# Graph attention, layer 0: 16 of 22 chunks of weights turned in blocks by VectorE, adjacency masks on ScalarE, ragged chunks of both heads turned together

## The chip, the cores and the metric

One core of one Trainium2 chip. The metric is the device time of one execution in microseconds, from runs of the whole program; the kernel before has a median of 2697.96 us over 3 runs (2696.49 to 2704.17).

## The reference, cut to what matters

Four graph layers over x (2708 x 512, float32) and an adjacency matrix (2708 x 2708, ones and zeros with ones on the diagonal). The change touches layer 0 alone, attention with 8 heads of 64:

```python
adj = jnp.maximum(adjacency_matrix, jnp.eye(n))
keys    = jnp.einsum('nj,hjk->hnk', node_matrix, Wks)      # queries, values alike
atts = jnp.einsum('hqk,hmk->hqm', queries, keys) / key_dim ** 0.5
atts = atts - 1e+16 * (1.0 - adj)[None, :, :]
atts = jax.nn.softmax(atts, axis=-1)
return jnp.einsum('hqm,hmk,hko->qo', atts, values, Wo)
```

Then `x = layernorm(x + layer(x, adj))`, and likewise for layers 1 to 3 (a normalised product with the adjacency, an additive attention, and a second normalised product). Layer 1 and layer 3 need the row sums of the adjacency, which layer 0 gathers on its way.

## The kernel before, in words

The 2708 rows are cut into 22 chunks of 128, the last with 20 rows. Keys (`KT`), values (`V`) and queries are computed first; the queries go to DRAM (`qtd`). Then one loop runs over 88 items: 22 chunks of query rows times 4 pairs of heads. `Pair` (L266) holds one item's state.

The keys of one item are taken in three batches, `ends = [0, 7, 14, 22]` in chunks, so 896, 896 and 916 columns. The steps of an item are:

- `scores(k, part)` (L283): half a batch; two TensorE products (one for each head) into PSUM `pss`, and for each head one VectorE pass (L306) that adds the mask from the adjacency tile, writes the scores to `s` and keeps the row maximum in `mx`. There are two `pss` banks for each head.
- `maxima` (L317): the negative row maximum `nm`, VectorE.
- `weights(k)` (L323): the exponential in place in `s` with its row sum, ScalarE, one instruction for each head (L328).
- The weights must then be turned, so that keys lie on partitions. For the first 14 chunks (`ND`) VectorE turns 32 x 32 blocks from `s` to `d` (`blocks`, L336) and `deal` (L348) moves the blocks to their partitions with four DMAs from `d` to `e` on SyncE's queue. To fit the order of keys that this gives, the rows of `V` of these chunks are permuted when they are projected (`xp`, GpSimd).
- `turn` (L359) does the last 8 chunks on TensorE: a transpose of each chunk of each head into PSUM `pst`, and copies to `pt` on ScalarE. The last, ragged chunk goes to `lastT`, which has zeros below its 20 rows.
- `values(m0, m1)` (L383): the products of the weights with `V` into PSUM `av`; after the 22nd chunk a copy to `ot` on ScalarE, and a store by GpSimd.

The adjacency of the next chunk of rows is loaded (`load_chunk`), summed by ScalarE (`row_sums`), and made into the mask (`mask`): VectorE puts ones on the diagonal where the batch holds it and turns 1 and 0 into 0 and -1e16. This is done in three of the four items of each chunk (`prep`).

The order of TensorE, VectorE and ScalarE inside the loop is the order in which the program writes it (`tc.manual_schedule`); SyncE's queue of DMAs is ordered by the framework. In one turn of the loop four items are in work: `new` gets scores, `cur` gets weights and is turned, `late` gets the products of the last batch and of the first, and `old` those of the second batch. `heads_sums` and `heads_rows` collect the reciprocals of the softmax sums twice in the whole loop.

The tiles `d` and `e` come from one pool `dep` with 3 buffers each; `s` has 5 buffers, `pt` 2, `pst` 3.

Of the kernel before, what the change touches and what calls it, by code (L numbers as in the profile page):

```python
# [15 lines left out]
P = 128  # L16
# [6 lines left out]
def kernel(  # L23
# [90 lines left out]


    NW = 3
    ends = [0, 7, 14, NC]
    ND = 14
    KD4 = P // 32
    SW = max(min(b * P, N) - a * P for a, b in zip(ends, ends[1:]))  # L120
    dgp = const.tile([P, NC, NW], F32, tag="dgp", name="dgp")
    nc.vector.memset(dgp, 0.0)
    HALF0 = NC // 2
# [7 lines left out]
    with ExitStack() as l0:  # L131
# [39 lines left out]
                a[:q, n0 : n0 + w], a[:q, n0 : n0 + w], AF.Copy, accum_out=dgp[:q, c, k : k + 1]  # L171
            )

        def mask(c, k):

            r0, q = rows(c)
            a = loaded[c][0]
            n0, w = batch(k)
            if n0 <= r0 < n0 + w:
                nc.vector.tensor_tensor(a[:q, r0 : r0 + q], a[:q, r0 : r0 + q], ident[:q, :q], ALU.max)  # L180
            nc.vector.tensor_scalar(a[:q, n0 : n0 + w], a[:q, n0 : n0 + w], 1.0, 1e16, ALU.subtract, ALU.mult)

        with tc.tile_pool(name="kvw", bufs=1) as kvw, tc.tile_pool(name="xTb", bufs=2) as xtp, tc.tile_pool(
            name="ps_0", bufs=4, space=PSUM
# [5 lines left out]
            for b in range(NB):  # L190
                n0, w = cols(b)
                xb = xtp.tile([P, KC, BLK], F32, tag="xb", name=f"xb{b}")
                load_rows(xb[:, :, :w], xT[:, n0 : n0 + w])
                if b == 0:
                    load_rows(wv_sb, wv)
                    load_rows(wq_sb, wq)

                def project_in(w_sb, p, name):
                    ps = ps_0.tile([P, BLK], F32, tag="t", name=name)
                    for k in range(KC):  # L200
                        nc.tensor.matmul(  # L201
                            ps[:, :w],
                            w_sb[:, k, p * P : (p + 1) * P],
                            xb[:, k, :w],
                            start=(k == 0),
                            stop=(k == KC - 1),
                        )
                    return ps

                for p in range(NP):  # L210
                    ps = project_in(wk_sb, p, f"psk{b}_{p}")
                    evac(KT[:, p, n0 : n0 + w], ps[:, :w])


                xp = xtp.tile([P, KC, BLK], F32, tag="xp", name=f"xp{b}", bufs=1)
                for c in chunks_of(b):
                    o, q = rows(c)[0] - n0, rows(c)[1]
                    src = xb[:, :, o : o + q]
                    dst = xp[:, :, o : o + q]
                    if c < ND:  # L220
                        src = src.rearrange("p k (i x) -> p k x i", i=KD4)
                        dst = dst.rearrange("p k (x i) -> p k x i", i=KD4)
                    nc.gpsimd.tensor_copy(dst, src)
                for c in chunks_of(b):
                    r0, q = rows(c)
                    ps = ps_0.tile([P, BLK], F32, tag="t", name=f"psv{c}")
                    for k in range(KC):
                        nc.tensor.matmul(  # L228
                            ps[:q, :],
                            xp[:, k, r0 - n0 : r0 - n0 + q],  # L230
                            wv_sb[:, k, :],
                            start=(k == 0),
                            stop=(k == KC - 1),
                        )
                    evac(V[:q, c, :], ps[:q, :])
                qb = xtp.tile([P, NP, BLK], F32, tag="qb", name=f"qb{b}")
                for p in range(NP):
                    ps = project_in(wq_sb, p, f"psq{b}_{p}")
                    nc.scalar.mul(qb[:, p, :w], ps[:, :w], QSCALE)
                for c in chunks_of(b):  # L240
                    r0, q = rows(c)
                    nc.gpsimd.dma_start(qtd[c], qb[:, :, r0 - n0 : r0 - n0 + q])
                if b == NB - 3:
                    for k in range(NW + 1):
                        load_chunk(0, k)
                    for k in range(NW):
                        row_sums(0, k)
                        mask(0, k)

            ga_sb = kvw.tile([P, D], F32, tag="ga", name="ga_sb")  # L250
# [9 lines left out]
        ps_a = l0.enter_context(tc.tile_pool(name="ps_a", bufs=1, space=PSUM, reuse_waits="tile"))  # L260
        ps_s = l0.enter_context(tc.tile_pool(name="ps_s", bufs=2, space=PSUM, reuse_waits="tile"))
        sp = l0.enter_context(tc.tile_pool(name="sp", bufs=5, reuse_waits="tile"))
        dep = l0.enter_context(tc.tile_pool(name="dep", bufs=3, reuse_waits="tile"))
        ptp = l0.enter_context(tc.tile_pool(name="ptp", bufs=2, reuse_waits="tile"))

        class Pair:  # L266

# [65 lines left out]
                        accum_out=smt[c // HALF0][:q, c % HALF0, 2 * p + j, k : k + 1],  # L333
                    )

            def blocks(self, k, j, m0, m1):  # L336

                if k not in self.D:
                    n = ends[k + 1] - ends[k]
                    self.D[k] = dep.tile([P, KD4, 2, n, 32], F32, tag="d", name=f"d{self.c}_{self.p}_{k}")  # L340
                b = 32 * self.groups
                m0, m1 = m0 - ends[k], m1 - ends[k]
                nc.vector.transpose(  # L343
                    self.D[k][:b, :, j, m0:m1].rearrange("p i m x -> p m i x"),
                    self.s[k][:b, j, m0 * P : m1 * P].rearrange("p (m i x) -> p m i x", i=KD4, x=32),
                )

            def deal(self, k):  # L348

                n = ends[k + 1] - ends[k]  # L350
                e = dep.tile([P, KD4, 2, n, 32], F32, tag="e", name=f"e{self.c}_{self.p}_{k}")
                for g in range(self.groups):
                    nc.sync.dma_start(
                        e[:, g].rearrange("p j m x -> p (j m x)"),
                        self.D[k][32 * g : 32 * g + 32].rearrange("p i j m x -> p i (j m x)"),
                    )
                self.E[ends[k]] = e

            def turn(self, m0, m1):  # L359

                c, p, q = self.c, self.p, self.q
                k = max(k for k in range(NW) if ends[k] <= m0)
                tiles = []
                for j in range(2):
                    pt = ps_t.tile([P, 4, P], F32, tag="t", name=f"pst{c}_{p}_{m0}_{j}")
                    n = sum(rows(m)[1] == P for m in range(m0, m1))
                    sb = ptp.tile([P, n, P], F32, tag=f"pt{n}", name=f"pt{c}_{p}_{m0}_{j}")
                    full = 0
                    for i, m in enumerate(range(m0, m1)):
                        mr = rows(m)[1]  # L370
                        o = (m - ends[k]) * P
                        nc.tensor.transpose(pt[:mr, i, :q], self.s[k][:q, j, o : o + mr], ident[:q, :q])  # L372
                        full += mr == P
                    if full:
                        nc.scalar.copy(sb[:, :full, :q], pt[:, :full, :q])  # L375
                    if full < m1 - m0:
                        mr = rows(m1 - 1)[1]
                        nc.scalar.copy(lastT[:mr, j, :q], pt[:mr, full, :q])
                    tiles.append(sb)
                for i, m in enumerate(range(m0, m1)):  # L380
                    self.pts[m] = (tiles, i)

            def values(self, m0, m1):  # L383
                c, p, q = self.c, self.p, self.q
# [2 lines left out]
                for m in range(m0, m1):  # L387
                    for j in range(2):
                        h = 2 * p + j
                        if m < ND:  # L390
                            f = max(f for f in self.E if f <= m)
                            x = self.E[f][:, :, j, m - f, :] if q == P else self.E[f][:, 0, j, m - f, :q]
                        else:
                            tiles, i = self.pts[m]
                            x = tiles[j][:, i, :q] if rows(m)[1] == P else lastT[:, j, :q]
                        nc.tensor.matmul(  # L396
                            self.av[j * KD : (j + 1) * KD, :q],
                            V[:, m, h * KD : (h + 1) * KD],
# [36 lines left out]
        with tc.manual_schedule(  # L435
            engines={mybir.EngineType.PE, mybir.EngineType.DVE, mybir.EngineType.Activation}
        ):
            for i in range(len(items) + 3):
# [9 lines left out]
                    new.scores(0, 0)  # L448
                    new.scores(0, 1)
                if old is not None:  # L450
                    old.values(7, ND)
                if cur is not None:
                    cur.weights(1)
                    cur.blocks(0, 0, 0, 7)
                    cur.blocks(0, 1, 0, 7)
                    cur.deal(0)
                if new is not None:
                    new.scores(1, 0)
                    new.scores(1, 1)
                if cur is not None:  # L460
                    cur.weights(2)
                if late is not None:
                    late.values(14, NC)
                    late.values(0, 7)
                if prep:
                    row_sums(c + 1, p - 1)
                if cur is not None:
                    cur.blocks(1, 0, 7, ND)
                    cur.blocks(1, 1, 7, ND)
                    cur.deal(1)  # L470
                if prep:
                    mask(c + 1, p - 1)
# [4 lines left out]
                if i in (HALF0 * NP + 2, len(items) + 1):  # L477
                    sums = heads_sums(i > HALF0 * NP + 2)
                if cur is not None:
                    cur.turn(14, 18)  # L480
                    cur.turn(18, NC)
                if i in (HALF0 * NP + 2, len(items) + 1):
                    heads_rows(*sums)
                old, late, cur = late, cur, new

# [598 lines left out]
```

## Time and profile before

| | |
|---|---|
| median of 3 runs | 2697.96 us |
| profiled execution, its own time | 2692.39 us |
| its span, first to last instruction | 2690.6 us |
| granted TensorE clock, mean | 0.992 |
| TensorE busy | 2630.5 us, 98% |
| VectorE busy | 1768.0 us, 66% |
| ScalarE busy | 1212.0 us, 45% |
| GpSimd busy | 330.5 us, 12% |
| 400 to 600 us: TensorE, VectorE, ScalarE busy | 200.0, 185.7, 152.3 us |
| 400 to 600 us: DMA share, GB/s | 0.72, 188 |

The page of a profile gives busy times of the engines, then the span in 40 slices with the busy share of each in tenths. Groups are listed by source line, engine and operation, with count, busy time, mean duration of one, and the idle time just before them with what ended it. The chain of waits follows the work that ended last back from the end, piece by piece: start, duration, engine, tile, line and number of instructions. A float32 product appears as two records, a transpose as one. PE is TensorE, PEld its loading of weights, DVE is VectorE, ACT ScalarE, POOL GpSimd, SP SyncE. The attention loop of layer 0 runs from about 233 to 1309 us of the span.

### The profile page before, as it was taken

To read this page: it belongs to the slowest core of one execution; us is meant where nothing else is said; L and a number is where in the kernel's file an instruction comes from. 1 tells how busy PE (TensorE), PEld (TensorE's weight loads), DVE (VectorE), ACT (ScalarE), POOL (GpSimd) and SP (SyncE) were. 2 spreads that over 40 slices of the span, in tenths; PEclk is the share of its full clock that TensorE was granted. 3 is DMA by queue.
4 is the path that set the end of the run, shared out by engine and by line. 5 is a ranking of instruction groups with operands and counts; after the bars stand their busy time and mean duration, and the time that the engine had idled before them with its cause. 6 is when DMAs were issued, how large, how long until landed. Compare 5 with 4: busy or idle time off the path is not lost.

```text
span 2690.6 us, 42656 instructions
## 1 busy us (share of the span) xinstructions
PE 2630.5 (98%) x15594; PEld 1484.2 (55%) x15594; DVE 1768.0 (66%) x4438; ACT 1212.0 (45%) x2570; POOL 330.5 (12%) x336
## 2 busy tenths in 40 slices
PE   8999999999999999999899999899999999999998
PEld 3445666666666666666547444444444464444445
DVE  2005999999999999999684677987776851111112
ACT  1114777777777777777311001565665530000001
POOL 1110000000000000001320000243333420000000
PEclk9999999999999999999899999999999999999999
DMA  5013777777767777776572444454433122222221
GB/s 193 32 52 76 206 182 186 202 186 190 198 177 204 184 181 207 181 186 148 151 234 66 131 123 140 126 165 127 138 114 100 49 59 69 77 78 77 78 67 41
DMA packets 199617, 361.98 MB, mean 135 GB/s; under 512 B 25160, under 2 KB 121752, under 8 KB 199408
## 3 DMA queue, kind: packets, MB, share of 16 engines
q1 hardware_dynamic: 193104, 342.52, 47.4%
q0 software_dynamic: 6304, 16.74, 1.8%
q8 instruction: 123, 2.02, 0.3%
q14 instruction: 86, 0.70, 0.1%
HBM read 186.36 MB, written 16.73 MB: 75 GB/s over the span
## 4 chain that ended last, share of the span: by engine, by line
PE 82%; issue 10%; DVE 4%; DMA 2%; ACT 1%; POOL 1%; SPq 1%; POOLq 0%; ACTq 0%; DVEq 0%
PE acc L641 19%; PE pss L298 16%; PE av L396 16%; PE acc L747 7%; PE pst L372 6%; PE pf L653 3%; PE psv L228 3%; PE psk L201 3%; PE psq L201 3%; PE po L587 2%; PE ph L733 2%; PE p L778 1%; PE pz L653 1%; DVE s L306 1%; DVE d L343 1%
## 5 line engine op out<-in xcount | busy, mean ns | idle before, releaser
L306 DVE CUSTOM_DVE_ANT_0 s<-pss,adj 128x448 f32<-128x448 f32 (+3 forms) x1056 | 596.3, 620 | 77.1 <-PE pss L298 75.4
L328 ACT ACTIVATE s<-s,nm 128x896 f32<-128x896 f32 (+1 forms) x528 | 546.9, 1038 | 12.6 <-DVE nm L321 12.4
L298 PE MATMUL pss<-KT,qt 64*128 64x448 f32 (+3 forms) x2112 | 478.0, 566 | 2.0 <-DVE mx L306 2.0
L641 PE MATMUL acc<-at,x 128*128 128x512 f32 (+1 forms) x1008 | 387.2, 542 | 0.0
L343 DVE STREAM_TRANSPOSE d<-s 128x896 f32<-128x896 f32 (+1 forms) x352 | 369.6, 1088 | 1.1 <-ACT s L328 1.1
L641 PE MATMUL acc<-pt,x 128*128 128x512 f32 (+1 forms) x880 | 336.6, 542 | 13.2 <-ACT pt L694 9.7
L396 PE MATMUL av<-e,V 128*64 128x128 f32 (+1 forms) x4928 | 300.3, 273 | 0.0
L396 PEld LDWEIGHTS av<-e,V 128*64 128x64 f32 x4928 | 267.9, 139 | 56.0 <-issue 45.5
L641 PEld LDWEIGHTS acc<-at,x 128*128 128x128 f32 x1008 | 180.8, 190 | 204.9 <-issue 202.6
L298 PEld LDWEIGHTS pss<-KT,qt 64*128 64x128 f32 (+1 forms) x2112 | 182.0, 182 | 156.0 <-issue 100.3
L641 PEld LDWEIGHTS acc<-pt,x 128*128 128x128 f32 x880 | 159.5, 194 | 189.9 <-issue 163.5
L375 ACT COPY pt<-pst 128x512 f32<-128x512 f32 (+3 forms) x352 | 165.4, 522 | 204.6 <-PE pst L372 204.2
L747 PE MATMUL acc<-at,h 128*128 128x512 f32 (+1 forms) x504 | 196.8, 543 | 0.0
L705 POOL TENSOR_TENSOR cs<-cs,pt 128x512 f32<-128x512 f32 (+2 forms) x110 | 156.6, 1423 | 202.5 <-ACT pt L694 195.9
L372 PEld LDWEIGHTS pst<-ident,s 128*128 128x128 f32 (+3 forms) x1408 | 140.4, 135 | 73.1 <-issue 58.3
L372 PE MATMUL pst<-ident,s 128*128 128x128 f32 (+3 forms) x1408 | 177.2, 277 | 1.7 <-ACT pt L375 1.4
L407 POOL DMA_DIRECT2D otd<-ot x88 | 47.4, 538 | 982.5 <-ACT ot L406 969.5
L396 PEld LDWEIGHTS av<-pt,V 128*64 128x64 f32 x2464 | 131.6, 139 | 60.5 <-ACT s L328 55.7
L692 DVE TENSOR_TENSOR pt<-pt,at 128x512 f32<-128x512 f32 (+2 forms) x132 | 107.0, 818 | 76.8 <-ACT pt L691 76.7
L93 ACT ACTIVATE ln_t<-lnve 128x1 f32<-128x1 f32 x88 | 17.7, 201 | 310.1 <-DVE lnve L107 309.9
L396 PE MATMUL av<-pt,V 128*64 128x128 f32 (+1 forms) x2464 | 152.3, 275 | 3.9 <-ACT ot L406 3.9
L1014 DVE TENSOR_TENSOR y<-z,x 128x512 f32<-128x512 f32 (+1 forms) x22 | 15.2, 692 | 211.0 <-ACT z L1012 210.9
(164 smaller groups left out, 2774.0 us busy)
## 6 DMA issues: line engine op xcount, KB each, us to landing
e<-d SPq DMA_DIRECT2D x680, 224.0 KB
at<-in_adjT_dram SPq DMA_DIRECT2D x315, 256.0 KB
a<-in_adj_dram SPq DMA_DIRECT2D x38, 677.0 KB
adj<-in_adj_dram SPq DMA_DIRECT2D x42, 448.0 KB
adj<-in_adj_dram SPq DMA_DIRECT2D x21, 458.0 KB
rb<-rs_d SPq DMA_DIRECT2D x44, 128.0 KB
qtd<-qb POOLq DMA_DIRECT2D x21, 256.0 KB, 5.2
qt<-qtd SPq DMA_DIRECT2D x21, 256.0 KB
```

The lines of the kernel that those rows point to most:

```text
L201: nc.tensor.matmul(ps[:, :w], w_sb[:, k, p * P : (p + 1) * P], xb[:, k, :w], start=(k == 0), stop=(k == KC - 1),)
L298: nc.tensor.matmul(pss[j][:q, :hw], qt[j * KD : (j + 1) * KD, p, :q], KT[j * KD : (j + 1) * KD, p, n0 + h0 : n0 + h0 + hw], start=True, st ...
L306: nc.vector.tensor_tensor_reduce(out=s[:q, j, h0 : h0 + hw], in0=pss[j][:q, :hw], in1=a[:q, n0 + h0 : n0 + h0 + hw], scale=1.0, scalar=LOW ...
L328: nc.scalar.activation(self.s[k][:q, j, :w], self.s[k][:q, j, :w], AF.Exp, bias=nm[j][:q], accum_out=smt[c // HALF0][:q, c % HALF0, 2 * p ...
L343: nc.vector.transpose(self.D[k][:b, :, j, m0:m1].rearrange("p i m x -> p m i x"), self.s[k][:b, j, m0 * P : m1 * P].rearrange("p (m i x) - ...
L372: nc.tensor.transpose(pt[:mr, i, :q], self.s[k][:q, j, o : o + mr], ident[:q, :q])
L375: nc.scalar.copy(sb[:, :full, :q], pt[:, :full, :q])
L396: nc.tensor.matmul(self.av[j * KD : (j + 1) * KD, :q], V[:, m, h * KD : (h + 1) * KD], x, start=(self.done == 0), stop=(self.done == NC - 1),)
L641: nc.tensor.matmul(acc[k][:, :w], last[0][g : g + mr, :] if m == NC - 1 else values[:mr, k * P : (k + 1) * P], moving[g : g + mr, :w], sta ...
L653: nc.tensor.matmul(pz[:q, :], yt[:, k, i * P : i * P + q], w_sb[:, k, :], start=(k == 0), stop=(k == KC - 1))
L705: nc.gpsimd.tensor_tensor(sums[:mr, :w], sums[:mr, :w], pt[:mr, :w], ALU.add)
L747: nc.tensor.matmul(acc[hc][:, :w], lastH[g : g + mr, :] if m == NC - 1 else H[m][:mr, hc * P : (hc + 1) * P], at[g : g + mr, :w], start=(m ...
```

## The change

- The batches become 8, 8 and 6 chunks (`ends = [0, 8, 16, NC]`): 1024, 1024 and 660 columns. `blocks` and `deal` now do 16 chunks, 8 to a batch; `turn` does the last 6.
- `turn` makes three PSUM tiles in place of four: four full chunks for each head, then one tile with the fifth full chunk of both heads and the ragged chunk of both heads. ScalarE copies it with one copy for the full chunks and one for `lastT`, where each head had its own.
- `mask` is an activation on ScalarE (Identity, scale 1e16, bias the tile `far` of -1e16). The ones on the diagonal stay on VectorE in a step of their own, `loops`.
- In the loop, `row_sums` moves ahead of `weights(1)`, `loops` comes after the first `blocks`, and `mask` stays after the second. `heads_rows` of the first half comes one turn later.
- `d` and `e` get pools of their own: `d` with 2 buffers where it had 3, `e` with 3 as before.

```diff
-    ends = [0, 7, 14, NC]
-    ND = 14
+    ends = [0, 8, 16, NC]
+    ND = ends[2]
...
+    far = const.tile([P, 1], F32, tag="far", name="far")
+    nc.vector.memset(far, -1e16)
...
-        def mask(c, k):
+        def loops(c, k):
...
             if n0 <= r0 < n0 + w:
                 nc.vector.tensor_tensor(a[:q, r0 : r0 + q], a[:q, r0 : r0 + q], ident[:q, :q], ALU.max)
-            nc.vector.tensor_scalar(a[:q, n0 : n0 + w], a[:q, n0 : n0 + w], 1.0, 1e16, ALU.subtract, ALU.mult)
+
+        def mask(c, k):
+
+            q = rows(c)[1]
+            n0, w = batch(k)
+            a = loaded[c][0][:q, n0 : n0 + w]
+            nc.scalar.activation(a, a, AF.Identity, scale=1e16, bias=far[:q])
...
-        dep = l0.enter_context(tc.tile_pool(name="dep", bufs=3, reuse_waits="tile"))
-        ptp = l0.enter_context(tc.tile_pool(name="ptp", bufs=2, reuse_waits="tile"))
+        dp = l0.enter_context(tc.tile_pool(name="dp", bufs=2, reuse_waits="tile"))
+        ep = l0.enter_context(tc.tile_pool(name="ep", bufs=3, reuse_waits="tile"))
+        ptp = l0.enter_context(tc.tile_pool(name="ptp", bufs=1, reuse_waits="tile"))
...
+            def turn(self):
 
                 c, p, q = self.c, self.p, self.q
...
+                last = NC - 2
+                o, mr = (NC - 1 - ND) * P, rows(NC - 1)[1]
+
+                def part(j, m):
+                    return self.s[2][:q, j, (m - ND) * P : (m - ND) * P + P]
+
                 for j in range(2):
...
+                    pt = ps_t.tile([P, last - ND, P], F32, tag="t", name=f"pst{c}_{p}_{j}")
+                    sb = ptp.tile([P, last - ND, P], F32, tag="pt", name=f"pt{c}_{p}_{j}", bufs=2)
+                    for m in range(ND, last):
+                        nc.tensor.transpose(pt[:, m - ND, :q], part(j, m), ident[:q, :q])
+                    nc.scalar.copy(sb[:, :, :q], pt[:, :, :q])
...
+                pt = ps_t.tile([P, 4, P], F32, tag="t", name=f"pst{c}_{p}_2")
+                sb = ptp.tile([P, 2, P], F32, tag="pt2", name=f"pt{c}_{p}_2")
+                for j in range(2):
+                    nc.tensor.transpose(pt[:, j, :q], part(j, last), ident[:q, :q])
+                for j in range(2):
+                    nc.tensor.transpose(pt[:mr, 2 + j, :q], self.s[2][:q, j, o : o + mr], ident[:q, :q])
+                nc.scalar.copy(sb[:, :, :q], pt[:, :2, :q])
+                nc.scalar.copy(lastT[:mr, :, :q], pt[:mr, 2:, :q])
...
                 if old is not None:
-                    old.values(7, ND)
+                    old.values(ends[1], ND)
+                if prep:
+                    row_sums(c + 1, p - 1)
                 if cur is not None:
                     cur.weights(1)
-                    cur.blocks(0, 0, 0, 7)
-                    cur.blocks(0, 1, 0, 7)
+                    cur.blocks(0, 0)
+                    cur.blocks(0, 1)
                     cur.deal(0)
+                if prep:
+                    loops(c + 1, p - 1)
...
                 if late is not None:
-                    late.values(14, NC)
-                    late.values(0, 7)
-                if prep:
-                    row_sums(c + 1, p - 1)
+                    late.values(ND, NC)
+                    late.values(0, ends[1])
                 if cur is not None:
-                    cur.blocks(1, 0, 7, ND)
-                    cur.blocks(1, 1, 7, ND)
+                    cur.blocks(1, 0)
+                    cur.blocks(1, 1)
                     cur.deal(1)
                 if prep:
                     mask(c + 1, p - 1)
...
                 if cur is not None:
-                    cur.turn(14, 18)
-                    cur.turn(18, NC)
-                if i in (HALF0 * NP + 2, len(items) + 1):
+                    cur.turn()
+                if i in (HALF0 * NP + 3, len(items) + 1):
                     heads_rows(*sums)
```

More of the change, by code (lines that the diff above doesn't have):

```diff
@@ L247 @@
                         row_sums(0, k)
+                        loops(0, k)
                         mask(0, k)
@@ L334, in weights, with blocks @@
                     )
-            def blocks(self, k, j, m0, m1):
+            def blocks(self, k, j):
                 if k not in self.D:
                     n = ends[k + 1] - ends[k]
-                    self.D[k] = dep.tile([P, KD4, 2, n, 32], F32, tag="d", name=f"d{self.c}_{self.p}_{k}")
+                    self.D[k] = dp.tile([P, KD4, 2, n, 32], F32, tag="d", name=f"d{self.c}_{self.p}_{k}")
                 b = 32 * self.groups
-                m0, m1 = m0 - ends[k], m1 - ends[k]
+                n = ends[k + 1] - ends[k]
                 nc.vector.transpose(
-                    self.D[k][:b, :, j, m0:m1].rearrange("p i m x -> p m i x"),
-                    self.s[k][:b, j, m0 * P : m1 * P].rearrange("p (m i x) -> p m i x", i=KD4, x=32),
+                    self.D[k][:b, :, j].rearrange("p i m x -> p m i x"),
+                    self.s[k][:b, j, : n * P].rearrange("p (m i x) -> p m i x", i=KD4, x=32),
                 )
@@ L350, in deal @@
                 n = ends[k + 1] - ends[k]
-                e = dep.tile([P, KD4, 2, n, 32], F32, tag="e", name=f"e{self.c}_{self.p}_{k}")
+                e = ep.tile([P, KD4, 2, n, 32], F32, tag="e", name=f"e{self.c}_{self.p}_{k}")
                 for g in range(self.groups):
@@ L357, in deal @@
                 self.E[ends[k]] = e
-            def turn(self, m0, m1):
+            def turn(self):
                 c, p, q = self.c, self.p, self.q
-                k = max(k for k in range(NW) if ends[k] <= m0)
-                tiles = []
+                last = NC - 2
+                o, mr = (NC - 1 - ND) * P, rows(NC - 1)[1]
+                def part(j, m):
+                    return self.s[2][:q, j, (m - ND) * P : (m - ND) * P + P]
                 for j in range(2):
[L365 to L381, printed above, removed]
@@ new lines, in turn @@
+                    pt = ps_t.tile([P, last - ND, P], F32, tag="t", name=f"pst{c}_{p}_{j}")
[3 more added lines that the diff above has]
+                    nc.scalar.copy(sb[:, :, :q], pt[:, :, :q])
+                    for m in range(ND, last):
+                        self.pts[m, j] = sb[:, m - ND, :q]
@@ L383, in values @@
+                for j in range(2):
+                    self.pts[last, j] = sb[:, j, :q]
+                    self.pts[NC - 1, j] = lastT[:, j, :q]
             def values(self, m0, m1):
@@ L393, in values @@
                         else:
-                            tiles, i = self.pts[m]
-                            x = tiles[j][:, i, :q] if rows(m)[1] == P else lastT[:, j, :q]
+                            x = self.pts[m, j]
                         nc.tensor.matmul(
```

## The prediction

> **What bounds the kernel now.** The page's first two parts place the stage: layer 0 fills roughly slices 4 to 19 of 40, and there TensorE and VectorE both show 9s. A 98% busy TensorE need not be the bound, so I read next the chain of waits in the middle of the stage; one period of it (one pair of heads of one row chunk):
>
> ```profile
> 505.26 1.98 PE pst L372 x16
> 507.23 1.71 PE pss L298 x8
> 508.94 1.68 PE av L396 x28
> 510.62 1.71 PE pss L298 x8
> 512.32 3.42 PE av L396 x60
> 515.75 1.74 PE pss L298 x8
> 517.49 1.98 PE pst L372 x16
> ```
>
> Every piece is TensorE and each begins where the last ended: 12.23 us, with no other engine and no wait in it. By kind: scores 5.16, values 5.10, transposes 1.98. Then the groups of the stretch 300 to 1100 us, split by shape (65.4 periods), and its waits:
>
> ```profile
> L343 DVE STREAM_TRANSPOSE d<-s 128x896 f32<-128x896 f32 x261 | 274.2, 1089 | 0.0
> L328 ACT ACTIVATE s<-s,nm 128x896 f32<-128x896 f32 x263 | 271.6, 1035 | 0.0
> L372 PE MATMUL pst<-ident,s 128*128 128x128 f32 x910 | 125.7, 281 | 0.0
> L375 ACT COPY pt<-pst 128x512 f32<-128x512 f32 x130 | 69.8, 589 | 155.2 <-PE pst L372 155.2
> L181 DVE TENSOR_SCALAR adj<-adj 128x896 f32<-128x896 f32 x33 | 19.8, 599 | 0.4
> ...
> DVE s L306 <- PE pss L298: 57.2, 66, 1.4
> ```
>
> VectorE is the near second: its only real idle time is 57.2 us, 0.87 us a pair, always at the first scores of a pair. ScalarE is busy about 9.3 us of 12.2 (the windows: 152.3 of 200) and waits for the transposes of TensorE. The timeline shows how the two leaders meet:
>
> ```profile
> 602.47 0.63 DVE L181 TENSOR_SCALAR adj<-adj 128x896 f32<-128x896 f32 x1
> 603.01 2.04 PE L372 MATMUL pst<-ident,s 128*128 128x128 f32 x16
> 604.98 1.77 PE L298 MATMUL pss<-KT,qt 64*128 64x448 f32 x8
> 605.23 0.28 DVE L321 TENSOR_REDUCE nm<-mx 128x1 f32<-128x6 f32 x2
> 606.03 0.62 DVE L306 CUSTOM_DVE_ANT_0 s<-pss,adj 128x448 f32<-128x448 f32 x1 [0.53 <-PE pss L298]
> 608.22 2.10 DVE L343 STREAM_TRANSPOSE d<-s 128x896 f32<-128x896 f32 x2
> ```
>
> VectorE has ended its maxima at 605.51 and idles to 606.03, because TensorE spent 603.01 to 604.98 on `turn`'s 16 transposes and only then began the scores. The first two periods of the stage, before TensorE has values to multiply, last 11.65 and 11.46 us (starts of the block transposes): what VectorE alone would set.
>
> **What the skill says.** VectorE: DVE Perf Modes, section on the TRN2 errata, gives fp32 two-tensor work as (N+151)/0.96 ns. 896 columns make 1091; the trace has 1089 for the block transpose, so I use that slope (1.04 ns a column). ScalarE: Activation LUTs, "What ACT_TABLE_LOAD costs", gives 280 ns + 0.833 ns a column with a bias operand, 93 ns of it overlapped back to back: 1026 for 896 against 1035 here. Its "Table sets" says that identity and copy are filler in every set, so the mask should bring no table load; before runs no Identity, so no line shows it. TensorE: Matmul & The Clock Gate, "PE-mode transpose", has about 275 ns for one transpose in a kernel; here 281 each, but 16 of them overlap into 1.98 us, so the price I use is 0.124 us.
>
> **The change, part by part**, for one pair.
> TensorE. `turn` covers 6 chunks for 2 heads, 12 transposes for 16: 4 x 0.124 = 0.495 us less, on the path. Scores keep 12 multiplications and 2 x 2708 columns; bursts of 448 and 458 columns (1.71, 1.74) give 0.87 ns a column and head pair, so 512 makes 1.93 a burst and 330 makes 1.29: 5.15 for 5.16. Values keep 88 records (32 + 56 for 28 + 60). Period 11.75.
> VectorE. 12 score passes: the spacing at 448 is 0.545 us, so 0.612 at 512 and 0.422 at 330: 6.58 before and after. Four block transposes go from 1.05 (2.10 for two) to 1.183: +0.53. This width isn't in the trace; bounds are 1.05 (no growth) and 1.25 (a fifth more), I take the slope. The mask, 0.53 in three pairs of four, goes; `loops` keeps 0.28 in one of four. Sum 6.58 + 4.73 + 0.28 = 11.59, or 11.87 with `loops`; it was 11.06, and 11.6 to 11.9 with the mask.
> ScalarE. Six exponentials keep their columns. Copies: from 2 of 512 columns, 2 of 384, 2 of 20 partitions to 2 of 512, one of 256, one of 20 partitions: about -0.7. Mask: an activation without accumulator, 1.04 (1024) or 0.74 (660) by the skill's price, bounds 0.6 (VectorE's) and 1.15; +0.7 on average. Near zero in sum, under slack of some 3 us. What matters is order: `row_sums`, 1.13 us, now precedes `weights(1)`.
>
> Stepping one pair from TensorE's start at 604.98: scores to 606.91, values to 608.77, scores to 610.70, values to 613.95, scores to 615.24, transposes to 616.73. VectorE: first pass 606.12, scores to 608.57, blocks to 610.94, scores to 613.39, blocks to 615.76, scores and maxima to 617.73; the next scores reach it at 617.87. It idles 0.14. The next score bank is free at 616.60, 0.13 before TensorE wants it. ScalarE: `weights(0)` ends about 608.05 (wanted 608.57), copy of `ot` 609.16, `row_sums` 610.29, `weights(1)` 612.57 (wanted 613.39), `weights(2)` 614.25 (wanted by the transposes 615.24), mask 615.3, copies from 615.97. Behind the moved `row_sums` stand both later exponentials and so the second block transpose, with 0.8 us to spare; its adjacency piece lands a whole pair earlier (624.9 to 627.8, wanted about 633). So TensorE stays ahead, but by a hair: the pair with `loops` is 0.14 over and hand-offs cost 0.1 to 0.2 each. I put 0 to 0.11 us a pair for that, 0.06 taken.
> SyncE and DMA. Still 8 deals a pair and the same loads; each deal grows from 224 to 256 KB. The DMA share of 0.74 becomes about 0.85 (deals are 79% of the bytes, the period 4% shorter). `d` has two buffers for three: `blocks(0)` now waits for the deal of one pair earlier. Matching landing records to issues, a batch of four deals has landed 6.9 us (median) after its block transpose, 8.05 at the 95th percentile. Scaled by bytes that is 7.9 and 9.2; the room is 11.8 - 2.4 = 9.4. So a few waits under 1 us, about +2 us in all (0 to 10).
> Nothing for: the projections' extra permuted chunks on GpSimd (TensorE's unbroken 13.7 us bursts there hide it), chunk 0's mask on ScalarE (14% busy there), the `far` memset. `heads_rows` moved a pair later removes one 1.7 us wait for `ri`, and its store on GpSimd's queue is wanted only after the stage; the end's first weight load gets a wait for ScalarE: -1 and +1.
>
> Sum: 86 pairs (the first two are VectorE's) x -0.495 = -42.6; +5 lag; +2 deals; 0 at the ends: -35.6. Against the profiled execution's own 2692.4 us (span 2690.6) this is 2656.8; the median shown is 5.6 above it, so 2662.4, said as **2662**. Its own range is 2652 (all 43 us and the small wait) to 2675.
>
> **The rivals.**
> VectorE becomes the bound. For it: only 0.14 us of slack. At 1.25 us a transpose it needs 11.93 with `loops` spread, period near 12.0: 86 x 0.22 = 19 us, 2679. At 1.33 it eats all: 2698. Against: the slope fits 448 and 896 columns within 1%. Chance 0.18, a third of it within 0.3%.
> The third `d` buffer was needed: slower. If a batch lands L after its transpose, VectorE can't start the next sooner, so the period is at least L + 2.4 + 0.1. It decides from L = 9.7; at 10.3 the period is 12.8 and 86 x 0.57 gives +49, 2747. For it: the DMA queues show 9s for most of a period, chunk loads (1.6 MB) push in front, bursts at 9.5 occur. Against: L must grow by 40% where bytes grow by 14%. Chance 0.08.
> ScalarE's order bites (`weights(0)` ending 0.2 us before VectorE wants it, `row_sums` late): 0.1 to 0.3 us a pair back, 2670 to 2688. Chance 0.10, mostly still faster.
> That the change isn't what it says is excluded by the instruction order: 12 transposes a pair, masks on ScalarE.
>
> **How the numbers follow.** The forecast has 0.64. A change under 0.3% (8 us) is about what this measurement can't tell from none. Faster: 0.64 + 0.12 + 0.08 = 0.84; same: 0.06 + 0.02 = 0.08; slower: 0.08. The range takes in the forecast's and most of the VectorE and ScalarE cases: 2649 to 2690.
>
> **What would show it.** Right: in the chain of waits `pst` x12 at 1.49 us, `pss` of 1.93, 1.93 and 1.29, period 11.75 to 11.85, still all TensorE; VectorE's wait for `pss` down from 0.87 us to 0.1 to 0.3 a pair; transposes at 1.22 us; no new wait of `d` for a DMA. Wrong: VectorE pieces in the chain, TensorE waiting for `mx` or `d`, block transposes waiting for `e`'s DMA or for exponentials, or a changed length outside layer 0.

## The result, and the profile after

| | before | after |
|---|---|---|
| median, measured side by side | 2697.22 us (4 runs) | 2662.1 us (4 runs, 2657.45 to 2663.44) |
| ratio, 95% interval | | 0.9867 [0.9838, 0.9895] |
| profiled execution, its span | 2692.39, 2690.6 us | 2662.35, 2660.6 us |
| transposes, scores, values of a pair | 1.98, 5.16, 5.10 us | 1.46, 5.15, 5.11 us |
| period, median | 12.23 us | 11.72 us |
| mean of 80 periods in the steady loop | 12.280 us | 11.855 us |
| last product of the attention ends | 1318.2 us | 1287.7 us |

The kernel is 35.1 us faster by the medians and 30.0 us by the two profiled executions. On another chip (e10 below) the ratio was 0.9891 [0.9869, 0.9913], 31 us. The period here and below is the distance between the starts of a pair's first block transposes; the first three and the last pairs are left out of the mean. Two profiles of the changed kernel, this one and e10's, differ by 0.033 us in the mean, 2.6 us over 80 pairs: differences between profiles that are smaller than this say nothing.

The chain of waits in the middle of layer 0, one period of the kernel after (start, duration, engine, tile, line, number):

```profile
510.91 1.02 PE pst L382 x8
511.94 0.22 PE pst L389 x2
512.16 0.22 PE pst L391 x2
512.38 1.92 PE pss L308 x8
514.29 1.90 PE av L410 x32
516.19 1.92 PE pss L308 x8
518.11 3.21 PE av L410 x56
521.32 1.31 PE pss L308 x8
522.63 1.02 PE pst L382 x8
```

It still holds nothing but TensorE, and each piece begins where the last ended: 522.63 - 510.91 = 11.72 us. Transposes are 1.46 us where they were 1.98; scores and values are what they were. The groups of the stretch 300 to 1060 us, by shape (count | busy us, mean ns | idle before):

```profile
L353 DVE STREAM_TRANSPOSE d<-s 128x1024 f32<-128x1024 f32 x256 | 302.9, 1222 | 8.5 <-DMA e<-d 4.4 <-ACT ot L420 2.7 <-issue 1.3
...
L383 ACT COPY pt<-pst 128x512 f32<-128x512 f32 x129 | 69.4, 589 | 92.1 <-PE pst L382 91.9
...
L189 ACT ACTIVATE adj<-adj,far 128x1024 f32<-128x1024 f32 x32 | 36.3, 1135 | 0.0
```

The block transpose takes 1222 ns, as the slope foretold, and it has idle time before it, which it didn't have before (0.0). The masks are on ScalarE at 1135 ns, and ScalarE still idles before its first copy: 92.1 us, 1.4 us a pair. The waits of VectorE (us in all, times, longest), over the attention loop:

```profile
DVE s L316 <- PE pss L308: 28.6, 60, 4.7
DVE d L353 <- DMA e<-d: 4.7, 6, 1.3
DVE d L353 <- ACT ot L420: 2.7, 4, 0.9
```

and the first of these lines before:

```profile
DVE s L306 <- PE pss L298: 75.4, 83, 4.5
```

New is that the block transposes wait: for the deals to be done with `d`. Two more lines put 2.1 us of such waits down to exponentials and 1.3 us to issue. What they really wait for comes out when the landing records of the deals are matched to their issues: from 280 to 1200 us, 14 block transposes idle for more than 0.1 us, and each of the 14 starts 0.12 to 0.18 us after the deals of one pair earlier have landed, whichever engine the list blames. Each comes 12 to 18 us after the loads of the next adjacency and queries were issued in one burst. One of these waits lies on the chain that ended last, at 713 us:

```profile
713.33 0.23 PE pst L391 x2
...
716.72 4.01 DMA e<-d
...
723.15 2.28 DVE d L353 x2
...
725.89 2.40 PE pss L308 x8
```

The chain leaves TensorE, goes through a deal on the DMA queue, and comes back by VectorE's scores and block transposes to TensorE, whose next scores take 2.40 us where they take 1.92 otherwise. The timeline of VectorE names the moment:

```profile
718.36 2.37 DVE L353 STREAM_TRANSPOSE d<-s 128x1024 f32<-128x1024 f32 x2 [1.19 <-DMA e<-d]
```

### The profile page after: what moved, and what is told of

Its sections match the earlier page's. It is cut to its first block, busy times and chain, and to the rows that moved or that the text cites. A ratio compares the mean times of both kernels' runs of the same rounds, so it can differ in the third digit from the quotient of the medians.

```text
span 2660.6 us, 41510 instructions
## 1 busy us (share of the span) xinstructions
PE 2599.1 (98%) x15242; PEld 1469.1 (55%) x15242; DVE 1772.1 (67%) x4373; ACT 1231.4 (46%) x2460; POOL 331.8 (12%) x336
## 3 DMA queue, kind: packets, MB, share of 16 engines
q8 instruction: 121, 1.98, 0.3%
## 4 chain that ended last, share of the span: by engine, by line
PE 76%; issue 10%; DVE 6%; DMA 3%; SPq 2%; ACT 2%; POOL 1%; POOLq 0%; DVEq 0%; ACTq 0%
PE acc L656 20%; PE pss L308 15%; PE av L410 14%; PE acc L762 7%; PE pf L668 3%; PE psv L236 3%; PE psk L209 3%; PE pst L382 3%; PE psq L209 3%; DVE s L316 2%; DVE d L353 1%; PE ph L748 1%; DMA e<-d 1%; PE p L793 1%; PE pz L668 1%
## 5 line engine op out<-in xcount | busy, mean ns | idle before, releaser
L316 DVE CUSTOM_DVE_ANT_0 s<-pss,adj 128x512 f32<-128x512 f32 (+3 forms) x1056 | 594.5, 618 | 29.9 <-PE pss L308 28.6
L338 ACT ACTIVATE s<-s,nm 128x1024 f32<-128x1024 f32 (+1 forms) x528 | 546.3, 1037 | 25.5 <-DVE nm L331 24.5
L308 PE MATMUL pss<-KT,qt 64*128 64x512 f32 (+3 forms) x2112 | 487.2, 568 | 7.3 <-DVE mx L316 7.0
L353 DVE STREAM_TRANSPOSE d<-s 128x1024 f32<-128x1024 f32 (+1 forms) x352 | 416.4, 1221 | 11.0 <-DMA e<-d 4.7
L410 PEld LDWEIGHTS av<-e,V 128*64 128x64 f32 x5632 | 306.7, 139 | 66.0 <-issue 35.5
L410 PE MATMUL av<-e,V 128*64 128x128 f32 (+1 forms) x5632 | 339.0, 273 | 0.0
L707 DVE TENSOR_TENSOR pt<-pt,at 128x512 f32<-128x512 f32 (+2 forms) x132 | 107.2, 819 | 75.4 <-ACT pt L706 75.4
L383 ACT COPY pt<-pst 128x512 f32<-128x512 f32 (+1 forms) x176 | 92.1, 572 | 128.2 <-PE pst L382 128.1
L762 PEld LDWEIGHTS acc<-at,h 128*128 128x128 f32 x504 | 90.2, 190 | 101.4 <-issue 99.2
L410 PEld LDWEIGHTS av<-pt,V 128*64 128x64 f32 x1760 | 93.6, 138 | 69.7 <-ACT adj L172 46.2
L709 ACT ACTIVATE pt<-pt 128x512 f32<-128x512 f32 (+2 forms) x132 | 76.2, 579 | 109.2 <-DVE pt L708 108.9
```

Source lines behind the costliest of these rows:

```text
L308: nc.tensor.matmul(pss[j][:q, :hw], qt[j * KD : (j + 1) * KD, p, :q], KT[j * KD : (j + 1) * KD, p, n0 + h0 : n0 + h0 + hw], start=True, st ...
L316: nc.vector.tensor_tensor_reduce(out=s[:q, j, h0 : h0 + hw], in0=pss[j][:q, :hw], in1=a[:q, n0 + h0 : n0 + h0 + hw], scale=1.0, scalar=LOW ...
L338: nc.scalar.activation(self.s[k][:q, j, :w], self.s[k][:q, j, :w], AF.Exp, bias=nm[j][:q], accum_out=smt[c // HALF0][:q, c % HALF0, 2 * p ...
L353: nc.vector.transpose(self.D[k][:b, :, j].rearrange("p i m x -> p m i x"), self.s[k][:b, j, : n * P].rearrange("p (m i x) -> p m i x", i=K ...
L383: nc.scalar.copy(sb[:, :, :q], pt[:, :, :q])
L410: nc.tensor.matmul(self.av[j * KD : (j + 1) * KD, :q], V[:, m, h * KD : (h + 1) * KD], x, start=(self.done == 0), stop=(self.done == NC - 1),)
```

## The experiments

Two things had to be told apart: where the gain comes from, and what keeps the changed kernel from TensorE's own 11.71 us a pair. Theory: the gain is TensorE's, the time of four transposes a pair, and the rest of the change (mask, shared tile, buffers) only keeps the other engines out of the way. Rivals: that the mask's move off VectorE or the shared tile (one PSUM tile for the ragged chunks of both heads) carried part of the gain. For what was lost against 11.71 us the candidates are late deals with two `d` buffers, the diagonal step (`loops`) and ScalarE's order. Ratios are to the kernel before on the same chip.

| | median us | ratio, 95% | mean of 80 periods | median period |
|---|---|---|---|---|
| e1 four more transposes | 2688.38 | 0.9980 [0.9971, 0.9988] | 12.164 | 12.15 |
| e2 mask back on VectorE | 2679.5 | 0.9943 [0.9922, 0.9964] | 12.047 | 11.98 |
| e3 kernel before, mask on ScalarE | 2689.08 | 0.9991 [0.9980, 1.0001] | 12.227 | 12.17 |
| e4 ragged tiles apart | 2674.89 | 0.9933 [0.9909, 0.9958] | 12.001 | 11.95 |
| e5 third `d` buffer | 2668.22 | 0.9904 [0.9889, 0.9919] | 11.790 | 11.80 |
| e6 loads spread | 2657.29 | 0.9863 [0.9847, 0.9880] | 11.748 | 11.71 |
| e7 no diagonal step | 2658.34 | 0.9869 [0.9854, 0.9883] | 11.781 | 11.71 |
| e8 loads spread, diagonal on GpSimd | 2653.88 | 0.9851 [0.9833, 0.9868] | 11.728 | 11.71 |
| e9 shared tile, six copies | 2661.27 | 0.9878 [0.9857, 0.9899] | 11.802 | 11.71 |
| e10 the changed kernel again | 2662.03 | 0.9891 [0.9869, 0.9913] | 11.822 | 11.72 |
| e11 e8 again | 2652.57 | 0.9848 [0.9828, 0.9869] | 11.745 | 11.71 |

e1 to e4 ran on one chip (before: 2693.97), e5 to e8 on another (2694.0), e9 to e11 on a third (2692.9). All but e3 start from the changed kernel. The two period columns are from the one profiled execution of each.

**e1: the four transposes put back**

```diff
-                for j in range(2):
+                for j in (0, 1, 0, 1, 0, 1):
                     nc.tensor.transpose(pt[:, j, :q], part(j, last), ident[:q, :q])
```

> The changed kernel, with four more TensorE transposes a pair: the two of chunk 20 are made three times instead of once, into the same PSUM tile, so that the pair has 16 transposes again as before the change. No copy and nothing of VectorE is added. Theory (TensorE's own time sets the period): its gapless period goes from 11.71 to about 12.15 us; the lag of VectorE behind it (0.15 us a pair in the mean of the changed kernel, 11.86) is then covered, so the mean goes to 12.15 to 12.2 and the time rises by 86 x 0.3 to 0.35 = 26 to 30 us, to 2688 to 2692. Rival (VectorE or ScalarE already sets the period, the transposes lie beside them): 0 to +5 us.

Measured: period 12.15, and 0.9980. The chain of waits of e1, the transposes of one pair:

```profile
505.88 1.02 PE pst L382 x8
506.90 0.66 PE pst L389 x6
507.55 0.22 PE pst L391 x2
```

The second piece has grown from 0.22 to 0.66 us: 0.44 for four, 0.11 us each, and the period by 0.43. Nearly the whole gain is gone with them, although mask, tiles, buffers and order are still the new ones. But e1 is not quite the kernel before: 12.15 against 12.23. That 0.08 is explained under e4.

**e2: the mask back on VectorE**

```diff
-            nc.scalar.activation(a, a, AF.Identity, scale=1e16, bias=far[:q])
+            nc.vector.tensor_scalar(a, a, 1.0, 1e16, ALU.subtract, ALU.mult)
```

> The changed kernel, with only the mask back on VectorE (a subtraction and a product, at the same place in the program). Theory: VectorE, at 11.6 us a pair with 0.1 us of idle left, gets 0.43 to 0.62 us in three pairs of four; it becomes the bound in these, about 12.2 us, mean 12.1: 86 x 0.26 = +23 us, to 2685; the chain of waits shows VectorE pieces. Rival (the idle time of VectorE swallows it): 0 to +8 us.

Measured: period 11.98, mean 12.047, 0.9943. VectorE's waits, first line:

```profile
DVE s L316 <- PE pss L308: 15.5, 31, 4.6
```

VectorE waits for scores half as long as in the changed kernel (28.6) and a fifth of what it did in the kernel before. In the chain of waits the mask (L189) now stands on the way to TensorE's scores, which stretch to 2.40 us behind it:

```profile
537.46 0.58 DVE adj L189
538.04 0.41 DVE s L316
538.51 2.40 PE pss L308 x8
```

About half of the gain is lost, somewhat less than was expected (2685). The mask's move was needed for the whole gain, then, but brings little by itself, as the next run shows.

**e3: the kernel before, with the mask on ScalarE**

```diff
-            nc.vector.tensor_scalar(a[:q, n0 : n0 + w], a[:q, n0 : n0 + w], 1.0, 1e16, ALU.subtract, ALU.mult)
+            nc.scalar.activation(a[:q, n0 : n0 + w], a[:q, n0 : n0 + w], AF.Identity, scale=1e16, bias=far[:q])
```

> The kernel before, with only the mask moved to ScalarE (the diagonal stays on VectorE, at its old place). Theory: TensorE sets 12.23 us there without a gap, so nothing is gained: 2697, within 3 us; VectorE's wait for scores grows from 75 us by the mask's 35 us. Rival (VectorE was a second bound already): 10 us or more faster.

Measured: 0.9991, with an interval that touches 1, so a gain of some 5 us at the most. VectorE's wait for scores grows from 75.4 to 99.7 us: most of the time freed there becomes waiting. Yet the median period fell from 12.23 to 12.17, with not one instruction less on TensorE. The chain of waits has the burst of 16 transposes in 1.92 us, where it took 1.98 before:

```profile
505.03 1.92 PE pst L374 x16
```

So there was idle time inside what the chain shows as an unbroken burst of transposes.

**e4: the ragged chunks of the heads in tiles of their own**

```diff
-                pt = ps_t.tile([P, 4, P], F32, tag="t", name=f"pst{c}_{p}_2")
-                sb = ptp.tile([P, 2, P], F32, tag="pt2", name=f"pt{c}_{p}_2")
                 for j in range(2):
+                    pt = ps_t.tile([P, 2, P], F32, tag="t", name=f"pst{c}_{p}_{2 + j}")
+                    sb = ptp.tile([P, P], F32, tag="pt2", name=f"pt{c}_{p}_{2 + j}", bufs=2)
...
-                nc.scalar.copy(sb[:, :, :q], pt[:, :2, :q])
-                nc.scalar.copy(lastT[:mr, :, :q], pt[:mr, 2:, :q])
+                    nc.scalar.copy(sb[:, :q], pt[:, 0, :q])
+                    nc.scalar.copy(lastT[:mr, j, :q], pt[:mr, 1, :q])
```

> The changed kernel, with the fifth full chunk and the ragged chunk of each head in a PSUM tile and two copies of its own again: 12 transposes as in the changed kernel, six copies by ScalarE for four, about 0.3 us more of ScalarE before the next exponentials. Theory (the gain comes from the four transposes fewer, the shared tile is worth little): 0 to +12 us, +5 the likeliest, since the first exponentials end about 0.2 us before VectorE wants them. Rival (turning the ragged chunks together is what pays): +25 us or more.

Measured: a period of 11.95 for 11.72, and 0.9933, which is 11 to 18 us slower by the two ratios of the changed kernel (0.9891 and 0.9867). The theory that the shared tile is worth little fails here. The chain of waits of e4, where it turns aside from TensorE in the middle of the transposes:

```profile
620.91 0.60 PE pst L382 x4
...
621.59 0.59 ACT pt L383
...
622.23 0.33 PE pst L389
622.56 0.11 PE pst L390
```

ScalarE's copy of the first tile stands between the third tile's transposes and the fourth's: there are three buffers for these tiles. The distances between starts of consecutive transposes, medians over the loop, tell it in each kernel. They are 0.165 us after the first transpose of a burst and then 0.109; in e4 those before and after the first transpose of the fourth tile are 0.294 and 0.165. The twelve begin within 1.496 us in e4 and 1.256 us in the changed kernel: 0.24 us a pair, and 86 x 0.24 = 20.6 us. Part of it comes back, for with the longer period fewer deals are late: over its own 11.95 us e4 loses 3.8 us in the 80 pairs, the changed kernel 9.0 to 11.6 over its 11.71. In the kernel before, the same place shows 0.130 and 0.165, 0.077 us over 2 x 0.109. This is e1's 0.08. In e3 it is 0.024, which is e3's fall of 0.05 us in the median period. That the copies of the first tile come earlier in e3, with less ahead of them on VectorE, would explain it; this was not followed further.

**e9: the same six copies, but one shared tile.** What was open in e4: the fourth tile, or the two extra copies on ScalarE?

```diff
                 for j in range(2):
                     nc.tensor.transpose(pt[:mr, 2 + j, :q], self.s[2][:q, j, o : o + mr], ident[:q, :q])
-                nc.scalar.copy(sb[:, :, :q], pt[:, :2, :q])
-                nc.scalar.copy(lastT[:mr, :, :q], pt[:mr, 2:, :q])
+                for j in range(2):
+                    sb = ptp.tile([P, P], F32, tag="pt2", name=f"pt{c}_{p}_{2 + j}", bufs=2)
+                    nc.scalar.copy(sb[:, :q], pt[:, j, :q])
+                    nc.scalar.copy(lastT[:mr, j, :q], pt[:mr, 2 + j, :q])
```

> The changed kernel with the ragged chunks of both heads in one shared tile as it has them, but copied out by four separate copies (two of 128 columns, two of 20 partitions), as with the tiles apart: six copies a pair for four, and still only three tiles. Theory (a fourth tile's first transpose waits for ScalarE's first copy, because TensorE has three buffers for these tiles; the copies as such are hidden in ScalarE's slack): the transposes begin 0.109 us apart throughout, the mean period of the changed kernel's own 11.85 us stays within 0.04, the whole 2662 within 4 us. Rival (the extra copies cost it, since ScalarE is late with the next weights): period near 12.0 as with the tiles apart, 2672 to 2677, and VectorE or TensorE waiting for ScalarE in the trace.

Measured: 2661.27, against 2662.03 for the changed kernel beside it. The chain of waits of e9:

```profile
614.58 1.02 PE pst L382 x8
615.61 0.22 PE pst L388 x2
615.82 0.22 PE pst L390 x2
```

The transposes are 0.109 us apart after the first (1.257 us from the first start to the last), as in the changed kernel, and the period is 11.71. So the two extra copies cost nothing that shows; the fourth tile in a pool of three buffers cost the 0.24 us.

**e5: a third `d` buffer.** To make room, `s` is split by width (three buffers of 1024 columns, two of 660, for five), and some small tiles and `ot` get fewer buffers.

```diff
-        dp = l0.enter_context(tc.tile_pool(name="dp", bufs=2, reuse_waits="tile"))
+        dp = l0.enter_context(tc.tile_pool(name="dp", bufs=3, reuse_waits="tile"))
...
-                    s = sp.tile([P, 2, SW], F32, tag="s", name=f"s{c}_{p}_{k}")
+                    s = sp.tile([P, 2, w], F32, tag=f"s{w}", name=f"s{c}_{p}_{k}", bufs=3 if k < 2 else 2)
```

> The changed kernel with three buffers for d. The room comes from s (three buffers of 1024 columns and two of 660 for five of 1024), one buffer for ot, and one for the temporaries of the degrees. Theory (what keeps the mean at 11.86 above TensorE's 11.71 is above all block transposes waiting for the deal of one pair earlier): these waits go, mean 11.75 to 11.79, -5 to -9 us, to about 2655. Rival (the waits that the profile puts down to ScalarE's copies are really ScalarE's): 0.

Measured: every wait of `d` is gone, and the mean period is 0.065 us under that of the changed kernel's profile, 5 us over the 80 pairs (0.032 and 2.6 us under e10's). But the periods now alternate between 11.71 and 11.81 us, 11.76 for the two, and the time is 2668.22, which is no gain. Waits of VectorE over the loop, and two lines of its timeline:

```profile
DVE s L316 <- PE pss L308: 14.3, 45, 4.7
DVE s L316 <- POOL s L301: 8.4, 5, 1.9
```

```profile
609.82 2.37 DVE L353 STREAM_TRANSPOSE d<-s 128x1024 f32<-128x1024 f32 x2
612.33 0.69 DVE L316 CUSTOM_DVE_ANT_0 s<-pss,adj 128x512 f32<-128x512 f32 x1
```

The scores after the first batch's block transposes start 0.14 us after these have ended, where after the second batch's they overlap; from start to start the median is 1.346 us for 1.126 in the changed kernel. By the count of buffers, with three wide ones these scores write the very tile that the transpose has just read. The trace agrees: just ahead of them VectorE waits for the semaphore that its own instructions count up, and in the changed kernel it has no such wait there. That is 0.22 us a pair on VectorE, whose waits for scores between 300 and 1060 us fall to 5.6 us from 17.1; in every second pair TensorE's first scores take 2.01 us for 1.92. In the ragged last chunk of rows VectorE waits 8.4 us for GpSimd to clear `s`: the time from the 84th pair to the last product is 67.6 us for 59.3. So e5 loses by the room that was made for the third `d`, and cannot say what the third `d` alone is worth.

**e6: the loads spread.** SyncE's queue joins the engines that keep the written order, so that the loads of the next adjacency and queries no longer pile up ahead of one pair's deals. (The expectations of e10 and e11 below call these the loads of weights.) In the changed kernel's trace all four are issued together; in e6's one comes in each pair, after its eight deals.

```diff
-            engines={mybir.EngineType.PE, mybir.EngineType.DVE, mybir.EngineType.Activation}
+            engines={mybir.EngineType.PE, mybir.EngineType.DVE, mybir.EngineType.Activation, mybir.EngineType.SP}
```

> The changed kernel with SyncE's queue in the program's order too: the three pieces of the next adjacency chunk and its queries are issued one in each pair, where the framework's order puts all four (1.6 MB) together ahead of one pair's deals. d keeps two buffers. Theory (deals are late only behind this burst): the late deals go, the pair of the burst falls from 12.1 to about 11.75, -5 to -8 us. Rival (d's waits are spread over all pairs, or aren't the cause): within 2 us.

Measured: by place in the group of four pairs, the periods are 11.713, 11.765, 11.778, 11.736; in the changed kernel 11.607, 11.930, 11.765, 12.118. The pair with the burst of loads is 0.38 us shorter; as the pair behind it no longer catches up (11.607 before, 11.713 now), the mean falls by 0.107. Of the waits of block transposes, over the loop, one line is left:

```profile
DVE d L353 <- ACT s L338: 1.3, 1, 1.3
```

Those for `e<-d`, and with them those put down to `ot` and to issue, are gone by an edit that touches only the order of SyncE's queue: they were late deals. A batch of four deals has landed 8.6 us after its transposes at the 95th percentile, 9.9 in the changed kernel (9.7 in e10). The 80 periods are 8.6 us shorter than in the changed kernel's profile and 5.9 us shorter than in e10's. In the timed runs 0.9863 is not to be told from the 0.9867 and 0.9891 of other chips.

**e7: without the ones on the diagonal**

```diff
-                if prep:
-                    loops(c + 1, p - 1)
```

and the same for row chunk 0.

> The changed kernel without the step that puts ones on the diagonal of the adjacency (left out; the diagonal of these inputs is already one). Theory: VectorE has no slack for its 0.27 us, once in each chunk, so 21 x 0.27 = 5.7 us go, to 2656; the pairs of 11.98 us become 11.71. Rival (the step lies in VectorE's idle time): 0.

Measured: a mean period of 11.781, which over 80 pairs is 5.9 us less than in the changed kernel's profile and 3.3 us less than in e10's, for 5.7 expected. The waits of `d` are shorter in this run too (6.3 us in all for 10.8), so not all of it need be the step. In the timed runs 0.9869 cannot be told from the changed kernel.

**e8 and e11: both remedies, against e10, the changed kernel.** The diagonal step goes to GpSimd as two operations on the 128 x 128 block (`off` is one minus the identity), with the loads spread as in e6.

```diff
-                nc.vector.tensor_tensor(a[:q, r0 : r0 + q], a[:q, r0 : r0 + q], ident[:q, :q], ALU.max)
+                d = a[:q, r0 : r0 + q]
+                nc.gpsimd.tensor_tensor(d, d, off[:q, :q], ALU.mult)
+                nc.gpsimd.tensor_tensor(d, d, ident[:q, :q], ALU.add)
```

> The changed kernel with both: SyncE's queue in program order, and the diagonal set by GpSimd (a product with one minus the identity and a sum with the identity, ahead of the mask). Theory: nearly the whole lag goes, mean 11.72 to 11.75, -9 to -12 us, about 2651. Rival (GpSimd's two steps come too late for the mask on ScalarE, or the lag has another cause): 0 to -5 us.

> The changed kernel once more, unaltered, on the same chip as the two beside it. Expected: ratio to before 0.987, mean period in layer 0 of 11.85 us, and the pair with the burst of weight loads near 12.1. It gives the yardstick for the other two.

> Both small remedies once more beside the changed kernel: the loads of weights spread over the pairs by SyncE running on, and the unit diagonal of the adjacency set on GpSimd. Theory (late deals and the diagonal step on VectorE are what the changed kernel lacks to TensorE's own 11.71 us): period 11.72 to 11.74, 8 to 11 us under the changed kernel beside it. Rival (this gain lies only in the profiled execution, whose deals happen to be late): no difference between the two in the timed runs.

Measured: e8 has a mean period of 11.728 and e11 of 11.745, TensorE's own being 11.71; e10, the changed kernel, has 11.822. Side by side on one chip, e11's runs lie from 2649.57 to 2654.21 and the changed kernel's from 2660.76 to 2668.15: 9.5 us between the medians. This is the fastest version here, 40 us under the kernel before. How much each remedy adds is not shown: against the changed kernel's profile the 80 periods lost 8.6 us with the loads spread, 5.9 without the diagonal step and 10.2 with both in e8, against e10's 5.9, 3.3 and 7.5. The single gains add up to more than the joint one, but by no more than two profiles of one kernel can differ.

## Why the prediction was right

**TensorE's gain: right, by two errors that cancel.** Predicted was 4 x 0.124 = 0.495 us a pair and a period of 11.75; measured 0.51 and 11.72. The price of a transpose was the mean of a burst of 16, and that burst had a stall in it. A transpose costs 0.109 us, so four cost 0.44 (e1); the other 0.08 is the wait for the fourth tile, which the shared tile removed. The prediction saw in the tile only fewer copies on ScalarE. Had the change kept separate tiles, the estimate would have been 0.22 us a pair too high (e4: 12.23 - 11.95 = 0.28 for 0.495). The scores came as foretold (1.92 and 1.31 us a burst for 1.93 and 1.29); the 0.87 ns used for them is the price of a column of one product, of which a burst has four, and not of a head pair.

**VectorE: right that it stays behind TensorE, with its work priced too high.** Predicted was 1.22 us for a block transpose alone; measured 1.222. The formula of the Trainium skill (VectorE: DVE Perf Modes, section on the TRN2 errata), which the page gives for the float32 addition of two tensors, makes (1024 + 151) / 0.96 = 1224 ns of it, and the trace agrees. Back to back 1.183 was put for each; from start to start they are 1.164 and 1.126. That is 0.15 us less for the four, and the work of a pair without `loops` comes out at 11.38 us (period less idle time, median) where 11.59 was put. Under TensorE's 11.71 this leaves 0.33 us, not 0.14. VectorE's wait for scores was 17.1 us between 300 and 1060 us, 0.27 us a pair, within the 0.1 to 0.3 foretold. The rival that VectorE becomes the bound did not come, but is near: with the mask back on it (e2) the period is 11.98. The mask's move was what kept the changed kernel out of it.

**ScalarE: right.** The mask took 1135 ns at 1024 columns and 833 at 660. The Trainium skill's formula (ScalarE: Activation LUTs, "What ACT_TABLE_LOAD costs": 280 ns + 0.833 ns a column) makes 1133 and 830; the prediction's 1.04 and 0.74 had taken off the overlap. No table load came with the mask: each trace, before and after, has one in all (1.28 us). ScalarE's work went from 9.4 to 9.6 us a pair, near zero as put. The rival that its order bites did not come: one wait of a block transpose for exponentials is left in e6, 1.3 us.

**Lag and deals: the mis-sized term.** Predicted was +5 us of hand-offs between TensorE and VectorE and +2 us (0 to 10) of deals. Measured over 11.71 us, the 80 periods of the changed kernel lose 11.6 us in one profile and 9.0 in another (e10). With the loads spread 3.0 are left, so 6.0 to 8.6 us hung on late deals, where +2 stood. With the diagonal step off VectorE as well 1.4 and 2.8 are left (e8 and e11), so hand-offs cost no more than about 3, where +5 stood. The two errors partly cancel in the sum. A sign that the prediction named for its being wrong did appear: block transposes waiting for `e`'s DMA, and VectorE in the chain at 713 us.

The mechanism and the room were right: the 14 waits of either profile follow batches that landed 9.4 us or more after their transposes. The step that failed is the scaling of the landing by bytes: the median came as foretold (7.9 us, from 6.9), the 95th percentile did not (9.9 and 9.7 for 9.2, from 8.05: up by more than a fifth where the bytes grew by a seventh). So 17 of 156 batches came later than the 9.4 us that there was room for. Why the tail grew more than the bytes was not tried by itself; that it comes with the burst of loads is shown by e6. The DMA share came as foretold, 0.85.

The rival of the third `d` buffer is this same mechanism at a sixth of its price or less (6.0 to 8.6 us for 49): waits of up to 1.3 us in some pairs, not a longer period throughout.

**The ends and the sum.** For the ends 0 was predicted. The loop gained 80 x 0.425 = 34.0 us and the span 30.0; the missing 4 lie in the first pairs (+1.0), the last ones (+1.6), the time ahead of the first pair (+0.9) and that behind the attention (+0.5). This last is 1372.4 and 1372.9 us, and 1369.2 to 1379.4 over all profiles here, so no cause is sought for it. The kernel before had two long periods, 14.18 us at the collecting of the sums in mid-loop and 14.51 at the start of the last chunk of rows; they are 12.50 and 13.16 now. Of the first, 1.95 us over the usual period became 0.8 with `heads_rows` a turn later, about the -1 that was put there (e3, with `heads_rows` in its old place, has 13.53).

The predicted sum of -35.6 against the profiled execution came to -30.0 there, and to -35.1 in the medians. The 2662 was met because the median shown of the kernel before stood 5.6 us above its profiled execution; on the other chips it stood nearer, and the gain was 31 us. That the number agrees to 0.1 us is luck, then; the working holds to about 5 us.

## What to carry to other kernels

Before a mean from a burst is used as the price of one instruction, look at the distances between its starts: here 0.08 of 1.98 us was a wait for a buffer that the chain of waits showed as work. A resource that is given away (the third `d` buffer) has to be judged by the tail of what holds it, in the pair where other loads pile up, not by the median scaled by bytes. And where two engines are within 0.3 us of each other, a part of a change may bring next to nothing alone (e3) and half of the gain may still depend on it (e2).

## What was not expected of the hardware

- Transposes of 128 x 128 float32 on TensorE begin 0.109 us apart when nothing holds them, while each is recorded as 273 to 280 ns. The Trainium skill's section "PE-mode transpose" (TensorE: Matmul & The Clock Gate) has about 275 ns for one of bf16 in a kernel; here that is the length of one, not its price in a burst.
- A score pass on VectorE that writes the tile which the block transpose before it has just read starts 1.346 us after that transpose's start, for 1.126 with another tile (e5). A dependence within one engine cost 0.22 us here, and the list of waits does not name it; it shows in the trace only as VectorE's wait for its own semaphore.
